# One layernorm tile moved beside a burst, and two blocks' softmax totals sent through DRAM, in a one-core attention and LoRA kernel

## The chip, the cores and the metric

The kernel runs on one core of a Trainium2 chip. Its time is the device time of that core in microseconds (us), as the median of several runs. A profile is one further execution, recorded by the hardware profiler; its times count from the start of its span. Five engines work side by side: TensorE (PE, with its weight loads as PEld), VectorE (DVE), ScalarE (ACT), GpSimd (POOL) and SyncE (SP), which here issues the DMAs. Each engine takes its instructions strictly in the order in which the program lists them.

## The reference

The input is four sequences of 1024 rows with 1024 columns, all in float32. Two steps follow each other:

```python
x = x + attention(layernorm(x), wq, wk, wv, wo)     # 32 heads of 32 columns, rotary q and k, causal softmax
x = x + lora(layernorm(x), route_w, A, Bw)          # one of 8 experts per row by its largest logit, rank 16

# inside attention, per head
probs = softmax(where(causal, q @ k.T / sqrt(32), lowest))
out = probs @ v
```

The weights are 1024x1024, the experts' matrices 8x16x1024 and 8x1024x16.

## The kernel before, in words

**Units.** The attention is cut into 32 units: four sequences `b` with eight groups `g` of four heads (4 x 32 = 128 columns). Unit u is group u % 8 of sequence u // 8, so unit 7 is the last of the first sequence. While unit u has its scores and softmax done, the projections (q, k, v) of unit u + 1 and, from the second sequence on, pieces of the output projection of the sequence before are put between. These go into a list of steps, `between[u]`, which is worked off during unit u. A step has a cost, in units of one 128x512 matmul; the loop over units (L1074) takes steps from the list, `todo`, until a slot's share of the cost is used (`fill`, `do_some`). A step of cost 0 has no matmul, and is done when its turn in the list comes. Nothing else decides the order: the program is written out in Python, and every engine follows it.

**Slots of a unit.** Queries are taken in 16 tiles t of 64 rows, in two blocks: block 0 is t = 0 to 7, block 1 is t = 8 to 15. `SLOTS` (L26) gives the order: score rounds for tiles 7 and 6, then 5, 4 and 3, then "second", then 2, 1, 0 and 9, then 15, 14, 13, 12, then "first", and then 11, 8 and 10. A score round (L417) runs its matmuls into the one PSUM tile `s` (L430), which ACT copies out (L441); POOL adds the causal mask (L444); DVE takes the maxima (L462) and joins the two halves of each row (L483); ACT takes the exponentials with their sums (L491); and DVE transposes the probabilities in place (L516). "second" (L1088) is `apply(u - 1, 1)`, the product of the probabilities of block 1 of the unit before with its values; "first" is `apply(u, 0)`. Such a product is a burst of 128 small matmuls per piece (L632), into the same PSUM tile `s`, so that the next score round can't start until DVE has read the burst's result (L652). Between the pieces of the second burst runs `meanwhile` (L1094): the transpose of v, and, where there is an entry `ahead_of[u]`, the moments of one layernorm tile of the next sequence (`find`). The entry's second half, the scaling of that tile (`scale`, L189), is run one slot later (L1113).

**Totals.** The softmax sums of a block are joined and inverted by `join_sums` (L555 to L566), and must then be spread over the rows on which the burst leaves its result. There are two ways. In the one (`by_turning` true), POOL widens the reciprocals into a 128x512 tile `by` (L569), PE transposes it in four matmuls (L603), and ACT copies it back (L604). In the other, DVE transposes 128x32 numbers (L576), four DMAs put them into DRAM (L582), and four more read them back, broadcast, into `by` (L587); both sets are put into `postponed`, with costs 2 and 5, and so are issued a few steps later, or at the latest by `spread_sums`. `by` has one buffer. In both ways L652 multiplies the burst's result by `by`.

**Layernorm ahead.** The eight 128-row tiles of the next sequence are normalized during this one (`Norm`, L247): `load`, `find` (two statistics instructions L178, an aggregate L180, an addition L182 on DVE, a power on POOL L184), `scale` (L189 on DVE), and `turn` (eight PE transposes L201, two copies L203 and L205 on ACT). For the second sequence, tiles 0 to 5 are found and scaled in units 1 to 6 by `ahead_of`; tile 6 and tile 7 are found and scaled in unit 6 by steps in `last_v`, which is `between[6]` (L923 to L930), tile 7 after steps 5 and 7 of the last v projection. Tiles 4 to 7 are turned in unit 7 by `change_steps` (L867).

Of the kernel before, what the change touches and what calls it, by code (L numbers as in the profile page):

```python
# [57 lines left out]
def weave(main, other):  # L58

    if not other:  # L60
        return list(main)
    out, taken = [], 0
    for n, step in enumerate(main):
        out.append(step)
        due = (n + 1) * len(other) // len(main)
        out += other[taken:due]
        taken = due
    return out + list(other[taken:])
# [3 lines left out]
def tile_preln_attn_then_top1_lora(  # L72
# [24 lines left out]
    NG = HEADS // HG  # L97
    NC = D // P
    NT = S // P
# [110 lines left out]
    units = [(b, g) for b in range(B) for g in range(NG)]  # L210
# [338 lines left out]
    def by_turning(u, blk):  # L549


        at = u + blk
        return at == 0 or at % NG == NG - 1 or at >= len(units) or (u, blk) == (NG - 2, 0)

    def join_sums(u, blk):  # L555

# [10 lines left out]
        if by_turning(u, blk):  # L567
            by = big.tile([P, TB, P], F32, tag="by", name=f"by_{u}_{blk}")
            nc.gpsimd.tensor_copy(  # L569
                by.rearrange("p t (h d) -> p t h d", d=HD),  # L570
                rec.rearrange("p h t -> p t h").unsqueeze(3).to_broadcast([P, TB, HG, HD]),
            )
            bys[u, blk] = by, None
            return
# [273 lines left out]
    def change_steps(u, norm, project, tail, held):  # L848

        p, h, turning, scaling = project, held, norm.turning, norm.scaling
        out, chains = [], []
        for n, tb in (("q", 0), ("k", 0), ("q", 1), ("k", 1), ("v", 0), ("v", 1)):
            chains += chain(u, n, tb)
        if p:
            turn, route, turn_hidden, adapt = tail
            find = norm.finding
            load_last = Step(lambda: norm.load(7), 0.0)
            out += [*h[:2], turn, *h[2:4], find(3), p[0], h[4], turning(2), h[5], p[1], route, scaling(3)]  # L860
            out += [find(4), h[6], p[2], h[7], p[3], turn_hidden, scaling(4), *p[4:6], adapt, load_last]
            out += [p[6], find(5), p[7], turning(3), scaling(5), *p[8:10], turning(4), *p[10:12]]
            chains = weave(chains[:-6], p[12:]) + chains[-6:]
            out += [*chains[:2], find(6), *chains[2:4], scaling(6), turning(5), *chains[4:6], find(7)]
            out += [*chains[6:8], scaling(7), turning(6), *chains[8:14], turning(7)]
            return out + chains[14:]
        for t, n in zip(range(TB, NT), (3, 4, 4, 4)):  # L867
            out += [*chains[:n], turning(t)]
            del chains[:n]
        return out + chains  # L870
# [4 lines left out]
    def behind(steps, at, step):  # L875

        steps.insert(steps.index(at) + 1, step)

    norms, ahead_of = {}, {}
    between, late_fetch = [], {}  # L880
    tail = []
    for u, (b, g) in enumerate(units):
        project, new_tail = [], []
        if b:
            fetch, (project,), new_tail = finish_steps(
                b - 1, g, "resident" if u == len(units) - 1 else "stream"
            )
            if g:
                apart = 3 if g + 1 == NG and u + 1 < len(units) else 8
                between[-1].insert(max(0, len(between[-1]) - apart), fetch)  # L890
            else:
                late_fetch[u] = fetch

        if u + 1 < len(units) and g + 1 == NG:
            last_v = between[-1]
            if b:
                norm = Norm(b + 1, {0: (2,), 2: (5,), 3: (6,)}, {3: "q", 4: "k", 6: "q"})
                load = [Step(lambda norm=norm, t=t: norm.load(t), 0.0) for t in range(2)]  # L900
                for at, step in (
                    (own["k", 0][0], load[0]),
                    (own["v", 0][0], norm.finding(0)),
                    (own["v", 0][1], load[1]),
                    (own["v", 0][2], norm.scaling(0)),
                    (own["v", 0][4], norm.finding(1)),
                    (own["v", 0][6], norm.turning(0)),
                    (own["v", 0][7], norm.scaling(1)),
                    (own["k", 1][2], norm.finding(2)),
                    (own["k", 1][3], norm.turning(1)),  # L910
                    (own["k", 1][5], norm.scaling(2)),
                ):
                    behind(last_v, at, step)
            else:

                norm = Norm(b + 1, {0: (7,)}, {5: "chunk", 6: "chunk"})
                for t in range(NG - 2):
                    ahead_of[t + 1] = (
                        lambda norm=norm, t=t: norm.find(t),
                        lambda norm=norm, t=t: norm.scale(t),  # L920
                    )
                    between[t].append(Step(lambda norm=norm, t=t: norm.load(t), 0.0))
                for at, step in (  # L923
                    (own["q", 0][0], Step(lambda norm=norm: norm.load(6), 0.0)),
                    (own["q", 1][0], norm.finding(6)),
                    (own["q", 1][3], norm.scaling(6)),
                    (own["v", 1][5], norm.finding(7)),
                    (own["v", 1][7], norm.scaling(7)),
                ):
                    behind(last_v, at, step)  # L930
                for t, at in enumerate((("k", 1), ("k", 1), ("k", 1), ("v", 1))):
                    behind(last_v, own[at][(1 + 3 * t) % NC], norm.turning(t))
            steps = change_steps(u + 1, norm, project, tail, held)
            norms[b + 1] = norm
        else:
            steps = []
            held = []
            if u + 1 < len(units):


                ends = g + 2 == NG and b + 1 < B
                own = {}
                for n, tb in ENDING if ends else USUAL:
                    own[n, tb] = chain(u + 1, n, tb)
                    if ends and b and (n, tb) == ("v", 1):
                        held = own[n, tb]
                    else:
                        steps += own[n, tb]
            if not steps:
                steps = list(project)  # L950
            elif b and not g:
                steps = steps[:36] + weave(steps[36:], project)
            else:
                steps = weave(steps[:-6], project) + steps[-6:]
            if u + 1 == len(units):
                new_tail6 = tail
            n = len(steps)
            for k, s in reversed(list(enumerate(tail))):
                steps.insert(6 + k * n // 7, s)
        between.append(steps)  # L960
        tail = new_tail
# [252 lines left out]
```

## Time and profile before

| | us |
|---|---|
| three runs | 2725.76, 2727.84, 2735.31 |
| median | 2727.84 |
| profiled execution | 2729.0 |
| its span, first to last instruction | 2727.2 |
| PE busy in the span | 2671.2 (98%) |
| DVE busy | 2141.2 (79%) |
| ACT busy | 1725.2 (63%) |
| POOL busy | 604.4 (22%) |
| mean granted PE clock | 0.995 |

The span is 1.8 us shorter than the execution. Unit 7 lies at some 515 to 592 us. The widening copies L569 of blocks (6, 0), (6, 1) and (7, 0), written as (unit, block), start at 498.58, 538.81 and 576.04 us. In a timeline a row gives the start, the time from the first to the last of a merged group, the engine, the line, the operation, the tiles and the count; in brackets stands the idle time before it, and who ended it.

### The profile page before, as it was taken

The numbers are of one execution on the slowest core, as the hardware profiler recorded it, in microseconds if no ns is written. First come the engines' busy times: TensorE is split into PE (matmuls) and PEld (weight loads), VectorE is DVE, ScalarE is ACT, GpSimd is POOL, SyncE is SP. The second block draws the span as 40 slices with busy tenths as digits, with TensorE's granted clock in tenths as the row PEclk, the third lists the DMA queues.
The fourth block names the chain that finished last, engine by engine and source line by source line (L and its number), as shares of the span: only waits on it lengthen the run. The fifth ranks groups of instructions, "written<-read, shape, count | busy, mean of one in ns | idle before, by whom it ended". The sixth has DMA issues, their size and how long they took to land.

```text
span 2727.2 us, 84063 instructions
## 1 busy us (share of the span) xinstructions
PE 2671.2 (98%) x35116; PEld 1305.0 (48%) x35116; DVE 2141.2 (79%) x4254; ACT 1725.2 (63%) x4980; POOL 604.4 (22%) x847
## 2 busy tenths in 40 slices
PE   8999999999999999989999999999999999999998
PEld 5444444444444544445444444444544444544445
DVE  4899999887777787887777878888778777777555
ACT  2878777876665676655666666766567666666421
POOL 2222222222221222222222222222212222222000
PEclk9999999999999999999999999999999999999999
DMA  3223233226555445652654444465354554446421
GB/s 118 60 72 74 75 77 84 53 56 174 139 140 131 126 131 155 167 157 61 163 161 134 135 131 132 136 187 142 83 159 135 159 136 133 131 132 185 123 69 53
DMA packets 465259, 332.19 MB, mean 122 GB/s; under 512 B 160496, under 2 KB 381936, under 8 KB 464880
## 3 DMA queue, kind: packets, MB, share of 16 engines
q1 hardware_dynamic: 464880, 326.83, 43.7%
q8 instruction: 276, 4.52, 0.7%
q14 instruction: 103, 0.84, 0.1%
HBM read 276.48 MB, written 50.24 MB: 120 GB/s over the span
## 4 chain that ended last, share of the span: by engine, by line
PE 79%; DVE 13%; ACT 3%; DMA 2%; POOL 1%; issue 1%; SPq 0%; POOLq 0%; DVEq 0%; ACTq 0%
PE po L749 15%; PE pq L337 14%; PE pk L337 13%; PE pv L337 11%; PE s L430 11%; PE av L632 8%; DVE top L462 4%; DVE pr L516 3%; PE ph L771 2%; PE pf L810 2%; ACT pr L491 1%; ACT pr L441 1%; DVE both L483 1%; PE pt_f L201 1%; DMA chunk<-in_wo 1%
## 5 line engine op out<-in xcount | busy, mean ns | idle before, releaser
L491 ACT ACTIVATE pr<-pr,both 128x256 f32<-128x256 f32 (+15 forms) x2048 | 1044.5, 519 | 55.5 <-DVE both L483 55.5
L441 ACT COPY pr<-s 128x640 f32<-128x640 f32 (+14 forms) x544 | 525.3, 1017 | 668.6 <-PE s L430 668.0
L462 DVE TENSOR_REDUCE top<-pr 128x2 f32<-128x960 f32 (+15 forms) x768 | 650.6, 893 | 256.8 <-POOL pr L444 256.2
L516 DVE STREAM_TRANSPOSE pr<-pr 128x1024 f32<-128x1024 f32 (+11 forms) x768 | 664.5, 907 | 33.7 <-ACT pr L491 30.4
L444 POOL TENSOR_TENSOR pr<-pr,causal_sb 128x128 f32<-128x128 f32 x512 | 239.0, 473 | 1152.2 <-ACT pr L441 1143.9
L337 PE MATMUL pv<-xnT,wv 128*128 128x512 f32 x1024 | 486.2, 602 | 0.0
L337 PE MATMUL pq<-xnT,wq 128*128 128x512 f32 x1008 | 479.1, 603 | 0.2 <-ACT xnT L203 0.2
L337 PE MATMUL pk<-xnT,wk 128*128 128x512 f32 x1008 | 476.8, 602 | 0.0
L430 PE MATMUL s<-kT,qT 32*32 32x256 f32 (+4 forms) x17408 | 393.8, 385 | 8.7 <-POOL pr L444 3.3
L491 ACT ACTIVATION_READ_ACCUMULATOR pr<-pr,both 128x1 f32 x2048 | 401.3, 196 | 0.0
L749 PE MATMUL po<-chunk,attn 128*128 128x512 f32 x736 | 379.7, 601 | 4.8 <-DMA chunk<-in_wo 4.8
L430 PEld LDWEIGHTS s<-kT,qT 32*32 32x32 f32 x17408 | 187.5, 103 | 266.2 <-issue 100.8
L337 PEld LDWEIGHTS pk<-xnT,wk 128*128 128x128 f32 x1008 | 181.2, 190 | 234.8 <-issue 234.5
L337 PEld LDWEIGHTS pq<-xnT,wq 128*128 128x128 f32 x1008 | 183.8, 192 | 226.1 <-issue 224.2
L337 PEld LDWEIGHTS pv<-xnT,wv 128*128 128x128 f32 x1024 | 185.6, 190 | 218.0 <-issue 217.2
L632 PE MATMUL av<-pr,vals 64*32 64x256 f32 (+3 forms) x12288 | 273.6, 321 | 6.9 <-DVE pr L516 6.5
L632 PEld LDWEIGHTS av<-pr,vals 64*32 64x32 f32 x12288 | 214.9, 106 | 115.5 <-issue 69.8
L483 DVE TENSOR_TENSOR both<-top 32x4 f32<-32x4 f32 (+3 forms) x1152 | 206.6, 179 | 23.8
L749 PEld LDWEIGHTS po<-chunk,attn 128*128 128x128 f32 x736 | 135.2, 190 | 170.1 <-issue 147.5
L652 DVE TENSOR_TENSOR at<-av,by 128x256 f32<-128x256 f32 x128 | 48.1, 417 | 110.0 <-PE av L632 71.5
L749 PE MATMUL po<-wo,attn 128*128 128x512 f32 x256 | 119.1, 607 | 2.3 <-DMA attn<-attn 2.3
L370 POOL TENSOR_TENSOR qT<-rawq,cos_sb 128x512 f32<-128x512 f32 x64 | 82.1, 1283 | 143.0 <-ACT rawq L363 143.0
(89 smaller groups left out, 1565.9 us busy)
## 6 DMA issues: line engine op xcount, KB each, us to landing
chunk<-in_wo SPq DMA_DIRECT2D x368, 256.0 KB, 3.8
vals<-vd SPq DMA_DIRECT2D x256, 128.0 KB, 4.3
x<-in_x SPq DMA_DIRECT2D x56, 512.0 KB, 5.0
wq<-in_wq SPq DMA_DIRECT2D x32, 512.0 KB, 4.7
wk<-in_wk SPq DMA_DIRECT2D x32, 512.0 KB, 3.9
wv<-in_wv SPq DMA_DIRECT2D x32, 512.0 KB, 4.2
vd<-vT SPq DMA_DIRECT2D x128, 128.0 KB, 4.5
out_y<-x SPq DMA_DIRECT2D x32, 512.0 KB, 2.6
```

The lines of the kernel that those rows point to most:

```text
L337: nc.tensor.matmul(at["p"], lhsT=wt[:, c, :], rhs=xnTs[b, tb][:, c, :], start=(c == 0), stop=(c == NC - 1),)
L370: nc.gpsimd.tensor_tensor(dst[:, cols], raw, cos_sb[:, cols], ALU.mult)
L430: nc.tensor.matmul(sc[i * SQ : (i + 1) * SQ, h, at : at + w].rearrange("p (j k) -> p j k", k=SQ), lhsT=of_q[rows, 2 * t + half], rhs=of_k[ ...
L441: nc.scalar.copy(pr[:, :, k0 : k0 + w], sc[:, :, at : at + w])
L444: nc.gpsimd.tensor_tensor(diagonal, diagonal, causal_sb.unsqueeze(1).to_broadcast([P, HG, SQ]), ALU.add)
L462: nc.vector.tensor_reduce(top[:, k, h : h + step], places[u, t][:, h : h + step, :], AX.X, ALU.max, negate=True,)
L483: nc.vector.tensor_tensor(dst[rows], src[rows], src[other], op)
L491: nc.scalar.activation(pr[:, h, :], pr[:, h, :], AF.Exp, bias=tops[u, t][:, h : h + 1], accum_out=dens[u, t // QT][:, t % QT, h : h + 1],)
L516: nc.vector.transpose(pr, pr)
L632: nc.tensor.matmul(avs[half][h * HD : (h + 1) * HD, t0:, :], lhsT=v[rows, j, h * HD : (h + 1) * HD], rhs=rhs, start=(j == 0), stop=(j == n ...
L749: nc.tensor.matmul(st["po"], lhsT=lhsT, rhs=rhs, start=(c == start), stop=(c == stop))
L771: nc.tensor.matmul(ph, lhsT=st["ynT"][:, c, :], rhs=w[:, c - i * RA, :], start=(c == 0), stop=(c == NC - 1),)
```

## The change

Two things are changed. In the first sequence (u < 8), only blocks (0, 0) and (6, 0) are still spread by turning; (6, 1) and (7, 0), which were too, now go by DRAM. And tile 7 of the second sequence's layernorm is no longer found and scaled by steps of `between[6]`, but by an entry `ahead_of[7]`: found between the two pieces of the burst (6, 1), in unit 7, and scaled in the slot after it. Its load stays where it was, after tile 0 is turned.

```diff
@@ by_turning(u, blk)
         at = u + blk
-        return at == 0 or at % NG == NG - 1 or at >= len(units) or (u, blk) == (NG - 2, 0)
+        if u < NG:
+            return (u, blk) in ((0, 0), (NG - 2, 0))
+        return at % NG == NG - 1 or at >= len(units)
@@ the loop that builds between[], b == 0, g + 1 == NG
                 norm = Norm(b + 1, {0: (7,)}, {5: "chunk", 6: "chunk"})
-                for t in range(NG - 2):
-                    ahead_of[t + 1] = (
+                for v, t in (*((t + 1, t) for t in range(NG - 2)), (NG - 1, NT - 1)):
+                    ahead_of[v] = (
                         lambda norm=norm, t=t: norm.find(t),
                         lambda norm=norm, t=t: norm.scale(t),
                     )
-                    between[t].append(Step(lambda norm=norm, t=t: norm.load(t), 0.0))
+                    if v < NG - 1:
+                        between[t].append(Step(lambda norm=norm, t=t: norm.load(t), 0.0))
                 for at, step in (
                     (own["q", 0][0], Step(lambda norm=norm: norm.load(6), 0.0)),
                     (own["q", 1][0], norm.finding(6)),
                     (own["q", 1][3], norm.scaling(6)),
-                    (own["v", 1][5], norm.finding(7)),
-                    (own["v", 1][7], norm.scaling(7)),
                 ):
```

## The prediction

> **What bounds the kernel now.** I read the page's busy times and chain first, then PE's waits by stretch, then the chain in order of time around unit 7, and then the timelines of PE, DVE, ACT, POOL and SP there. Units 4 and 5 serve as patterns, since they already do what unit 7 will do.
>
> ```profile
> PE 2671.2 (98%) x35116; PEld 1305.0 (48%) x35116; DVE 2141.2 (79%) x4254; ACT 1725.2 (63%) x4980; POOL 604.4 (22%) x847
> PE 79%; DVE 13%; ACT 3%; DMA 2%; POOL 1%; issue 1%; SPq 0%; POOLq 0%; DVEq 0%; ACTq 0%
> ```
>
> PE is the bound, so something off PE gains only where PE waits. Of the 13% of the chain that DVE has, a part lies where the change is. PE's timeline shows it:
>
> ```profile
> 520.28 1.44 PE L430 MATMUL s<-kT,qT 32*32 32x256 f32 x64 [2.70 <-ACT pr L441]
> 521.65 4.52 PE L337 MATMUL pq<-xnT,wq 128*128 128x512 f32 x6
> ...
> 532.09 1.04 PE L201 MATMUL pt_a<-eye_sb,x 128*128 128x128 f32 x8
> 537.04 6.43 PE L632 MATMUL av<-pr,vals 64*32 64x256 f32 x128 [3.91 <-DVE pr L516]
> ```
>
> PE stands 3.91 us until DVE has transposed block (6, 1), and the burst's first piece then takes 6.43 us. In unit 5 the same piece takes 3.68 us (start 329.92, no idle). The excess of 2.75 us is the clock, by the table of windows (third column from the end):
>
> ```profile
> 534.00:537.00 3.00, 0.00 (x0) 0.00 (x0) 2.90 (x7) 2.41 (x9) 0.00 (x0) 0.72 0.00 0
> 537.00:540.00 3.00, 2.96 (x53) 2.24 (x61) 2.84 (x8) 2.49 (x10) 0.61 (x1) 0.50 0.00 0
> 540.00:543.00 3.00, 3.00 (x80) 2.54 (x68) 2.89 (x8) 0.99 (x4) 0.00 (x0) 0.65 0.03 5
> ```
>
> What DVE does before it lets PE go:
>
> ```profile
> 525.87 0.67 DVE L483 TENSOR_TENSOR both<-top 32x8 f32<-32x8 f32 x4
> 526.57 1.29 DVE L178 BATCH_NORM_STATS2 st_a<-x 128x6 f32<-128x512 f32 x2
> 527.89 0.21 DVE L180 BATCH_NORM_AGGREGATE mv_a<-st_a 128x2 f32<-128x12 f32 x1
> 528.14 0.15 DVE L182 TENSOR_SCALAR ve_a<-mv_a 128x1 f32<-128x1 f32 x1
> 528.96 0.94 DVE L189 TENSOR_SCALAR x<-x,mv_a,rstd_a 128x1024 f32<-128x1024 f32 x1 [0.67 <-POOL rstd_a L184]
> 529.82 1.82 DVE L516 STREAM_TRANSPOSE pr<-pr 128x768 f32<-128x768 f32 x2
> 531.57 2.16 DVE L462 TENSOR_REDUCE top<-pr 128x4 f32<-128x1024 f32 x2
> 533.77 0.73 DVE L483 TENSOR_TENSOR both<-top 32x8 f32<-32x8 f32 x4
> 534.52 3.02 DVE L516 STREAM_TRANSPOSE pr<-pr 128x704 f32<-128x704 f32 x4
> ```
>
> The five middle instructions are tile 7's layernorm, with a trip to POOL, and DVE has no other idle time from there to the burst. They lie on the chain.
>
> **The change, part by part.**
>
> *Layernorm taken from before the burst.* DVE's next work starts at 526.57 instead of 529.82, so 3.25 us earlier. Its inputs allow it: ACT ended tile 11's exponentials at 523.5, and POOL's masks for tiles 7 and 6, which stood behind the waiting power (POOL idle 7.61 us until 528.37), can run at about 526. Carrying on: transposes of tile 11 to 528.3, maxima to 530.5, their joining to 531.2, the two transposes of tile 10 (about 0.83 each of the 3.02) to 532.9, the first of tile 8 to 533.6. The last needs tile 8's fourth exponential, which ACT gives only at 533.7, behind an eviction that has no part in the change:
>
> ```profile
> 531.45 1.85 ACT L441 COPY pr<-s 128x768 f32<-128x768 f32 x3
> 533.19 0.55 ACT L491 ACTIVATE pr<-pr,both 128x288 f32<-128x288 f32 x1
> ```
>
> So the last transpose ends at about 534.5 instead of 537.54: 3.0 of the 3.25 us arrive, and ACT is the next limit. PE is free at 533.13, starts its first heads at 533.6 and waits shortly for the last two until 534.5, in all 1.0 to 1.4 us idle instead of 3.91. At 3.5 us for the rest the piece ends at 538.0 instead of 543.47: **5.5 us**, of which 3.0 is the earlier transpose and 2.5 the clock.
>
> The clock's part rests on a rule, and here row and rule differ. The Trainium skill (TensorE: Matmul & The Clock Gate, the table "Why this matters for your kernels") asks for no PE-idle gap over about 3 us, since one idle window drops the clock to half. In this trace the gap of 2.70 us at 517.6 was enough: granted clock 0.50 from 522 to 524, and six matmuls took 4.52 us where six otherwise take 2.84. By rule and row alike a remaining gap of 1.0 to 1.4 us keeps the full clock (gaps of 0.97 and 1.31 us, at 475 and 408, had no such stretch). But if only half of the shift arrived, leaving some 2.4 us, the rule would still give 1.5 + 2.5 = 4.0 us and the row only 1.5. I take the row for the range.
>
> *The same layernorm put beside the burst.* Five DVE instructions (1.29 + 0.21 + 0.15, later 0.94) and POOL's power (0.55). DVE after the burst's start, by the durations of before: sums and reciprocal to 535.6, the new 128x32 transpose (0.21) to 535.8, maxima 2.21 and joining 0.69 to 538.8, transpose of tile 7 to 540.0, of v to 541.2, the moments to 542.9, shuffle and product to 544.4. PE meanwhile: 2 + 4 matmuls to 540.8, second piece to 543.1, 2 matmuls, a turn and 4 matmuls (0.86 + 0.88 + 1.72) to 546.5, where the score round of tiles 2, 1, 0, 9 needs DVE to have read the burst: L652 from 544.4 to 545.2, 1.3 us in time. What hides the moments is idle time that DVE had here before (1.27 + 2.76 + 3.20 us between 543.9 and 555.6). Scaling ends at about 548.1; tile 7 is turned at 550.4 (before: 556.32). Cost nothing; if the cover were gone, at most the 2.6 us themselves.
>
> *Totals of (6, 1) by DRAM.* Removed: POOL 0.61, four PE transposes, ACT 0.59, and DVE's 2.76 us wait for that copy. The Trainium skill (same page, "Part 4: PE-mode transpose") measured about 275 ns for one transpose in a kernel's context. The row has the same, 273 ns, but the four overlap: in the chain they take 0.59 us. By the rule eight of them are 2.2 us, by the row 1.2; I take the row, **0.6 us** a block. Added: eight DMAs on SP, 0.41 us of issue each. Put and get stand behind the unit-8 wk load (issued 517.61) and ahead of the attn store, which waits for L652 anyway; SP is otherwise idle from 518 to 550. How long the trip takes, unit 5 shows:
>
> ```profile
> 330.83 1.71 SPq L582 DMA_DIRECT2D recs<-recT  x4
> 333.56 2.25 SPq L587 DMA_DIRECT2D by<-recs  x4
> 339.89 0.34 SPq L665 DMA_DIRECT2D attn<-at  x1
> ```
>
> From the small transpose's end (330.8) to the last landing (335.8 + 2.2 = 338.0) are 7.2 us; in unit 6 it is 8.1. From 535.8 that is 543.0 to 543.9, before DVE comes to L652 at 544.4. Cost nothing.
>
> *Totals of (7, 0) by DRAM.* Again 0.6 us of PE. The small transpose ends at 576.1 of the old clock, landing at 583.3 to 584.2; DVE comes to L652 at 585.2, busy until then. Behind put and get on SP now stands the wq load of unit 9, issued some 5 us later than 576.74; with 4.7 us to land it is there by 586.5, and its first matmul was at 597.92.
>
> After that PE has no idle time in unit 7 or 8's start, so what is gained stays. **Sum: 5.5 + 0.6 + 0.6 = 6.7 us.** Against the profiled execution's 2729.0 (span 2727.2, 1.8 outside) that is 2722.3. The median of the runs is 1.2 lower, so 2721.1; I forecast **2721.5**.
>
> **Bounds.** PE idle before the burst (3.91), clock excess (2.75) and transposes (1.2) give at most 7.9 us in this place. At least the transposes and half of the shift: 1.2 + 1.5 = 2.7. Later half-clock stretches (the trace's clock record falls to half for 3.4 us at four more places, all after 1200 us) depend on where a gap falls against the gate's windows; shifting all by 6.7 us may add or remove one or two, some 1.7 us each (half of 3.4), either way.
>
> **The rivals.**
> - *ACT or the clock keeps part of it (20%)*: ACT's fourth exponential comes later than I put it, PE still idles over 2 us and the clock still falls. 2.7 to 4 us gained, about 2724.5. For it: ACT already sets the end, 0.2 us after DVE would. Against: its work before that point is not touched.
> - *Everything comes, and a later half-clock stretch goes as well (10%)*: 9 to 11 us, about 2718.
> - *It does not act at all (5%)*: PE is 98% busy, and what DVE gains is waited for elsewhere; only transposes are saved, 2727. Against: the chain runs through these very instructions.
> - *Slower (6%)*: DVE waits in L652 for the DRAM trip of (6, 1), behind it wait the scaling of tile 7 and the tops, and PE's next score round. It decides against the change from the moment that the landing is later than 552.4 (546.5 less 0.75 for L652, plus the 6.7 gained), 16.6 us after the small transpose. With every issue and landing at the worst of all 212 (1.58 and 3.5, 1.81 and 3.8 us): 4 x 1.58 + 3.5 + 4 x 1.81 + 3.8 = 20.9, landing 556.7: 11.0 us of wait less 6.7 gained, 4.3 us slower than before, about 2732. Against: 53 such trips in the trace, and PE waited at most 0.97 us for one.
> - The forecast itself: 59%.
>
> **Numbers.** The range is 2715.5 to 2727: from the third case's deeper part to the lower bound of the first with the runs' scatter of some us. Over 0.5% (13.6 us, about what a measurement of this kernel can tell from no change) would be below 2714.2 or above 2741.5; no single mechanism above reaches either. Faster 0.06, same 0.91, slower 0.03.
>
> **What would show it.** After: PE's idle before the first piece of (6, 1) at most 1.5 us instead of 3.91, that piece at 3.7 to 4.4 us, no stretch of half clock there; DVE goes from L483 straight to L516; the wait of L652 for ACT's copy is gone with no DMA wait over 1 us in its place; units 0 to 6 as before. Wrong, if the clock still falls at 535, if PE waits for DVE at the score round near 546, or if the span moves by more than this place does.

## The result and the profile after

| | before | after |
|---|---|---|
| median, us | 2729.38 (7 runs, 2725.76 to 2735.31) | 2721.73 (7 runs, 2716.47 to 2724.26) |
| profiled execution, its span | 2729.0, 2727.2 | 2722.25, 2720.5 |
| mean granted PE clock | 0.995 | 0.997 |

The ratio of after to before is 0.997, with a 95% interval of 0.996 to 0.998: 5.5 to 10.9 us less. That is within half a per cent, as forecast, and 0.2 us from the forecast of 2721.5. The text below shows that the terms of the sum came less exactly than that.

In the changed kernel the lines behind L553 stand two further down: L632 is L634, L652 is L654. PE's timeline at the same place, and DVE's ahead of it:

```profile
521.54 1.62 PE L430 MATMUL s<-kT,qT 32*32 32x256 f32 x64 [2.69 <-ACT pr L441]
523.09 4.32 PE L337 MATMUL pq<-xnT,wq 128*128 128x512 f32 x6
...
533.32 1.04 PE L201 MATMUL pt_a<-eye_sb,x 128*128 128x128 f32 x8
535.32 0.64 PE L634 MATMUL av<-pr,vals 64*32 64x256 f32 x8 [0.96 <-DVE pr L516]
536.20 3.66 PE L634 MATMUL av<-pr,vals 64*32 64x256 f32 x120 [0.25 <-DVE pr L516]
```

```profile
527.12 0.92 DVE L483 TENSOR_TENSOR both<-top 32x8 f32<-32x8 f32 x4
528.08 1.84 DVE L516 STREAM_TRANSPOSE pr<-pr 128x768 f32<-128x768 f32 x2
529.84 2.17 DVE L462 TENSOR_REDUCE top<-pr 128x4 f32<-128x1024 f32 x2
532.04 0.73 DVE L483 TENSOR_TENSOR both<-top 32x8 f32<-32x8 f32 x4
532.80 2.37 DVE L516 STREAM_TRANSPOSE pr<-pr 128x704 f32<-128x704 f32 x3
535.37 0.78 DVE L516 STREAM_TRANSPOSE pr<-pr 128x576 f32<-128x576 f32 x1 [0.20 <-ACT pr L491]
```

The layernorm is gone from before the burst, DVE goes straight on, and the last transpose waits 0.20 us for ACT's fourth exponential: ACT is the next limit, as forecast. POOL's masks for tiles 7 and 6, which stood behind the waiting power until 528.88 before, begin at 526.26. PE's idle time at the burst is 0.96 + 0.25 us instead of 3.91, and the first piece runs at full clock (granted clock 1.00 from 535 to 540). After the burst began:

```profile
542.72 1.25 DVE L178 BATCH_NORM_STATS2 st_a<-x 128x6 f32<-128x512 f32 x2
544.00 0.21 DVE L180 BATCH_NORM_AGGREGATE mv_a<-st_a 128x2 f32<-128x12 f32 x1
544.24 0.15 DVE L182 TENSOR_SCALAR ve_a<-mv_a 128x1 f32<-128x1 f32 x1
...
545.09 1.72 DVE L371 TENSOR_TENSOR swapq<-swapq,sin_sb 128x512 f32<-128x512 f32 x1
546.73 0.74 DVE L654 TENSOR_TENSOR at<-av,by 128x256 f32<-128x256 f32 x2
```

L654 shows no wait in brackets: the DRAM trip of (6, 1) was there before DVE was. PE's next score round starts at 548.49, 1.0 us after L654 ends, with no idle time either.

**A measure for the place.** Two executions don't reach 508 us at the same time (the changed one is 1.27 us later there, with nothing changed so far). So I count from the score round of tile 11 in unit 6 to that of unit 7, start to start on PE, and call it the stretch: 586.37 - 508.25 = 78.12 us before, 581.99 - 509.52 = 72.47 after. **5.65 us are won in this place.** The two rounds, before and then after:

```profile
508.25 1.49 PE L430 MATMUL s<-kT,qT 32*32 32x384 f32 x64
...
586.37 1.49 PE L430 MATMUL s<-kT,qT 32*32 32x384 f32 x64
```

```profile
509.52 1.48 PE L430 MATMUL s<-kT,qT 32*32 32x384 f32 x64
...
581.99 1.50 PE L430 MATMUL s<-kT,qT 32*32 32x384 f32 x64
```

The profiled spans differ by 6.7: 1.27 was lost ahead of it and 2.3 won behind it, where the clock's record has four spells of half clock before (at 1201, 2559, 2645 and 2686 us) and two after (1881 and 2680). The last section has more on these.

### The profile page after: what moved, and what is told of

The parts are those of the page before. It is cut to its first block, busy times and chain, and to the rows that moved or that the text cites. A ratio compares the mean times of both kernels' runs of the same rounds, so it can differ in the third digit from the quotient of the medians.

```text
span 2720.5 us, 84063 instructions
## 1 busy us (share of the span) xinstructions
PE 2666.9 (98%) x35108; PEld 1302.4 (48%) x35108; DVE 2143.7 (79%) x4256; ACT 1723.5 (63%) x4978; POOL 601.4 (22%) x845
## 3 DMA queue, kind: packets, MB, share of 16 engines
q8 instruction: 276, 4.52, 0.7%
## 4 chain that ended last, share of the span: by engine, by line
PE 79%; DVE 13%; DMA 3%; ACT 3%; POOL 1%; issue 1%; SPq 1%; POOLq 0%; DVEq 0%; ACTq 0%
PE po L751 15%; PE pq L337 14%; PE pk L337 13%; PE pv L337 11%; PE s L430 11%; PE av L634 8%; DVE top L462 4%; DVE pr L516 3%; PE ph L773 2%; PE pf L812 2%; DMA chunk<-in_wo 2%; DVE both L483 1%; ACT pr L441 1%; ACT pr L491 1%; PE pt_f L201 1%
## 5 line engine op out<-in xcount | busy, mean ns | idle before, releaser
L634 PE MATMUL av<-pr,vals 64*32 64x256 f32 (+3 forms) x12288 | 272.0, 319 | 4.6 <-DVE pr L516 3.8
L634 PEld LDWEIGHTS av<-pr,vals 64*32 64x32 f32 x12288 | 214.1, 106 | 112.3 <-issue 66.4
L483 DVE TENSOR_TENSOR both<-top 32x4 f32<-32x4 f32 (+3 forms) x1152 | 207.8, 180 | 23.8
L654 DVE TENSOR_TENSOR at<-av,by 128x256 f32<-128x256 f32 x128 | 48.2, 418 | 108.7 <-PE av L634 70.4
L375 POOL TENSOR_TENSOR qT<-qT,swapq 128x512 f32<-128x512 f32 x64 | 81.6, 1274 | 140.0 <-DVE swapq L371 140.0
```

The lines of the kernel that those rows point to most:

```text
L375: nc.gpsimd.tensor_tensor(dst[:, cols], dst[:, cols], other, ALU.add)
L483: nc.vector.tensor_tensor(dst[rows], src[rows], src[other], op)
L634: nc.tensor.matmul(avs[half][h * HD : (h + 1) * HD, t0:, :], lhsT=v[rows, j, h * HD : (h + 1) * HD], rhs=rhs, start=(j == 0), stop=(j == n ...
```

## The experiments

Theory: the layernorm lay on DVE's chain before the burst; most of the gain is its moving, part of it through the clock. Rival 1: the totals by DRAM do it. Rival 2: the first piece is slow for another reason than the clock. Rival 3: the layernorm still costs something in its new place. The ratios are to runs of the kernel before that were taken alongside on the same chip.

**Layernorm alone** (`by_turning` as before):

```diff
-        if u < NG:
-            return (u, blk) in ((0, 0), (NG - 2, 0))
-        return at % NG == NG - 1 or at >= len(units)
+        return at == 0 or at % NG == NG - 1 or at >= len(units) or (u, blk) == (NG - 2, 0)
```

> Layernorm of tile 7 moved beside the burst; all totals spread as before. The measure is the stretch from the score round of tile 11 in unit 6 to that in unit 7 (start to start on PE): 78.1 us before, 72.5 after the whole change. Theory (the layernorm lay on DVE's chain before the burst): stretch near 73.5, so 4.6 of the 5.6 us, no half clock at the burst of (6, 1). Rival (the totals do it: no wait of L652 for ACT's copy): stretch stays at 77 to 78. Median: 4 to 7 us under before by the theory, 0 to 1 by the rival.

Measured: stretch 73.21 us, 4.91 less; ratio 0.9973 (0.9963 to 0.9982). The piece again takes 3.7 us at full clock:

```profile
531.87 0.64 PE L632 MATMUL av<-pr,vals 64*32 64x256 f32 x8 [0.95 <-DVE pr L516]
532.75 3.66 PE L632 MATMUL av<-pr,vals 64*32 64x256 f32 x120 [0.25 <-DVE pr L516]
```

**Totals alone** (the kernel before with the new `by_turning`):

> Only the totals of (6, 1) and (7, 0) by DRAM; tile 7 normalized before the burst as before. Theory: only the eight transposes go, 0.6 us a block, stretch near 77.0, idle before the burst still 3.9 us and the clock still at half there. Rival (the totals do it): stretch near 73. If the DRAM trip costs a wait, the stretch is over 78. Median within 2 us of before by the theory.

Measured: stretch 77.41, 0.71 less; ratio 0.9992 (0.9986 to 0.9998), so 0.5 to 3.8 us. Rival 1 falls. That 4.91 and 0.71 add up to nearly 5.65 is partly chance: of the 0.71, 0.53 come from a first piece that ended earlier (34.69 us into the stretch instead of 35.22), with one spell of half clock of 3.41 us there instead of 6.83, and a new wait at (7, 0) takes 0.29 back. A cleaner price of the totals is the layernorm alone against the whole change, where the clock holds in both: 73.21 - 72.47 = 0.74 us. The DRAM way also shows its risk here, at (7, 0):

```profile
578.67 3.15 SPq L589 DMA_DIRECT2D by<-recs  x4
```

```profile
535.89 5.91 PE L634 MATMUL av<-pr,vals 64*32 64x256 f32 x128 [4.15 <-DVE pr L516]
...
584.52 1.48 PE L430 MATMUL s<-kT,qT 32*32 32x384 f32 x64 [0.61 <-DVE at L654]
```

The four reads took 3.15 us to issue instead of 1.70 in the whole change, and PE waited 0.61 us at the score round behind them. Slow issue is not needed for such a wait: in three other runs (half of the shift, and the totals of (6, 0) by DRAM with no and with four spare matmuls) the four reads took 1.70 us, and PE still waited 0.32, 0.16 and 0.17 us at that round. The piece of (6, 1) keeps its idle time and its half clock.

**Tile 7's layernorm left out** (that tile is projected unnormalized):

```diff
+                    if v == NG - 1:
+                        ahead_of[v] = (
+                            lambda norm=norm: setattr(norm, "found", NT),
+                            lambda norm=norm: setattr(norm, "scaled", NT),
+                        )
```

> The whole change with the moments and the scaling of the second sequence's tile 7 left out altogether, so that tile goes into the projections unnormalized. It prices the layernorm in its new place. Theory (idle time of DVE hides it): stretch within 0.3 us of the whole change's 72.5, median within 1.5 us of it. Rival (it still costs its 2.6 us on DVE, which paces PE's next score round): stretch near 70.

Measured: stretch 72.43; median 2721.99, ratio 0.9971 (0.9961 to 0.9982). In its new place the layernorm costs 0.04 us (72.47 - 72.43). DVE instead waits 0.94 us for the DRAM trip, so the time that hides it is there either way; rival 3 falls.

```profile
544.34 0.76 DVE L654 TENSOR_TENSOR at<-av,by 128x256 f32<-128x256 f32 x2 [0.94 <-DMA by<-recs]
```

**Half of the shift** (the moments stay before the burst, the scaling moves):

```diff
                     (own["q", 1][3], norm.scaling(6)),
+                    (own["v", 1][5], norm.finding(7)),
```

> As the whole change, but the moments of tile 7 (1.65 us on DVE) stay before the burst, and only the scaling with its wait for POOL goes beside it, so half of the shift. PE's idle before the burst near 2.2 us. If the clock only falls after a gap over about 3 us, as the rule has it, no half clock at the burst, and a stretch near 74. If a gap of 2.1 to 2.7 us is enough, as the row at 517 us has it, half clock there and a stretch near 76.5. Median 4 under before by the rule, 1 to 3 by the row.

Measured: stretch 75.91; ratio 0.9978 (0.9972 to 0.9985). But PE's idle time was 4.47, not 2.2:

```profile
518.12 1.44 PE L430 MATMUL s<-kT,qT 32*32 32x256 f32 x64 [2.70 <-ACT pr L441]
519.49 2.84 PE L337 MATMUL pq<-xnT,wq 128*128 128x512 f32 x6
...
533.76 5.79 PE L634 MATMUL av<-pr,vals 64*32 64x256 f32 x128 [4.47 <-ACT pr L491]
```

The gap of 2.70 us at 515 to 518 was this time *not* followed by half clock (six matmuls in 2.84 us), so PE was at the burst earlier and waited longer. The row names ACT as the releaser, but DVE too worked without a gap until its last transpose ended at 534.27; the burst starts 27.67 us into the stretch, 1.1 earlier than before. As a test of the two readings of the clock it misses. It shows something else: PE's idle time before the burst is not a size of its own. The softmax work on DVE and ACT sets when the burst starts, and PE's arrival varies with the clock before.

**Spare matmuls where PE waits, in the kernel before**:

```diff
         avs, pieces = value_pieces(u, blk)
+        for k in range(7 if (u, blk) == (NG - 2, 1) else 0):
+            if k == 0:
+                spare = bank([P, HALF], f"spare_{u}_{blk}")
+            nc.tensor.matmul(spare, lhsT=eye_sb, rhs=cos_sb[:, :HALF], start=True, stop=True)
```

> The kernel before with seven spare 128x512 matmuls (some 3.1 us, into a bank that nothing reads) where PE waits before the first piece of (6, 1), so that PE is busy there while DVE's chain is untouched. If the slow first piece (6.4 us instead of 3.7) is the clock's doing, that piece takes 3.7 to 4.2 us, no half clock there, and the stretch is 78.1 - 2.5 = 75.6. If it is slow for another reason (the transposes of the last two heads, bank or memory contention), it stays at 5.8 to 6.4 and the stretch at 78. Median 2 to 3 under before by the first.

```profile
532.79 6.17 PE L1057 MATMUL spare<-cos_sb,eye_sb 128*128 128x512 f32 x14
538.90 3.69 PE L632 MATMUL av<-pr,vals 64*32 64x256 f32 x128
```

Measured: the piece takes 3.69 us, which speaks against rival 2, though the piece also started later. But a float32 matmul is two rows in the profile; seven took 6.17 us and held the burst up by some 1.8. The stretch is 77.16, ratio 0.9992 (0.9985 to 0.9999).

**Three spare matmuls instead of seven:**

> The kernel before with three spare 128x512 matmuls (six rows of the profile, 2.7 us; seven were 6.2 us and held the burst up) in PE's idle 3.9 to 5.5 us ahead of the first piece of (6, 1). By the clock theory the idle time left is 1.2 us after a half-clock stretch at 520, or some 2.8 without one; in the first case the burst starts 28.8 us into the stretch as before, takes 3.7 us, and the stretch is 78.1 - 2.7 = 75.4. If the slow piece is not the clock's doing, 78.

```profile
531.31 2.74 PE L1057 MATMUL spare<-cos_sb,eye_sb 128*128 128x512 f32 x6
535.41 4.22 PE L632 MATMUL av<-pr,vals 64*32 64x256 f32 x128 [1.36 <-DVE pr L516]
```

Measured: the burst starts 28.78 us into the stretch, as before (28.79), and its first piece ends at 33.00 instead of 35.22: **the clock alone is 2.2 us** here, and with the same start rival 2 falls. The stretch is 76.94 and not the 75.4 expected: the piece takes 4.22 us, not 3.7, and PE stands still once more for 0.87 us inside the burst of (7, 0), with no releaser in the profile. Ratio 0.9984 (0.9977 to 0.9991).

**A better version?** The totals of (6, 0) by DRAM too:

```diff
-            return (u, blk) in ((0, 0), (NG - 2, 0))
+            return (u, blk) in ((0, 0),)
```

> The whole change, and the totals of (6, 0) by DRAM too. Theory: the gap of 2.7 us before the score round of tile 10 starts with DVE's wait of 2.3 us for ACT's copy of (6, 0); by DRAM the landing comes 7.5 us after the small transpose, 1.0 to 1.5 us before ACT's copy would, so the gap shrinks to some 1.5 us and the half clock after it goes: 0.5 + 1.2 + 1.7 = 2.5 to 3.5 us under the whole change, about 9 under before. Rival (the trip is no faster than the copy, and DVE waits as long for the DMA): 0 to 1 us under the whole change.

Measured: the gap before tile 10's round shrinks to 1.11 us and the burst of (6, 1) starts 1.6 us earlier in the stretch; but PE, no longer slowed, waits 2.57 us for it, and now the clock falls there:

```profile
518.76 1.43 PE L430 MATMUL s<-kT,qT 32*32 32x256 f32 x64 [1.11 <-POOL pr L444]
520.12 2.84 PE L337 MATMUL pq<-xnT,wq 128*128 128x512 f32 x6
...
532.49 5.77 PE L634 MATMUL av<-pr,vals 64*32 64x256 f32 x128 [2.57 <-DVE pr L516]
```

Stretch 72.14; ratio 0.9968 (0.9955 to 0.998), not to be told from the whole change. The median of its five runs, 2718.5, lies some 3 us lower, as expected, but the stretch only 0.3. So I filled the waits ahead of the first pieces of (0, 1) and (6, 1), first with four spare matmuls each, then with two.

**With four spare matmuls:**

> The whole change, the totals of (6, 0) by DRAM as well, and four spare matmuls (1.8 us) ahead of the first pieces of (0, 1) and (6, 1), where PE waits 2.6 us for DVE. If the earlier start by the one is spoilt by the half clock that it brings (first piece 5.8 us there), the first piece takes 3.7 us, the stretch is 72.1 - 2.1 = 70.0, unit 1 gains 2 us more, and the median is 3 to 5 us under the whole change, with less scatter. If not, it is as the run without the spare matmuls.

Measured: stretch 73.79, where 70.0 was expected; ratio 0.9972 (0.996 to 0.9984). Four took 3.6 us and held the burst up by some 2; and this time DVE waited for the trip of (6, 0):

```profile
503.24 0.76 DVE L654 TENSOR_TENSOR at<-av,by 128x256 f32<-128x256 f32 x2 [2.87 <-DMA by<-recs]
```

**With two spare matmuls:**

> The whole change, the totals of (6, 0) by DRAM, and two spare matmuls (1.8 us) ahead of the first pieces of (0, 1) and (6, 1). Theory: no window of 3.4 us is idle for 1.9 us there any more, so both first pieces take 3.7 to 4 us; stretch 72.1 - 2.1 = 70.0 if the landing of (6, 0) is in time as in the one trace, 71.5 if it is 1.5 us late as in the other. Median 2 to 5 us under the whole change, 8 to 11 under before. If the spare matmuls hold up the bursts again, as the whole change.

Measured: no half clock in units 1 to 7, stretch 71.61; ratio 0.997 (0.9957 to 0.9983). The stretch is the best of all; the median, 2720.82, is not 2 to 5 us under that of the whole change (2721.73) as expected.

**The whole change once more:**

> The whole change once more, beside the other three on one chip. Median 5 to 8 us under before. The stretch 72.5 if the gap before (6, 1), near 1.2 us, keeps the clock again; 74 to 75 if the clock falls this time.

Measured: stretch 72.48; ratio 0.9976 (0.9966 to 0.9986). Yet PE's idle time before the burst was 2.60, not 1.2, and the clock held, both there and after the gap of 2.69 us at 517:

```profile
519.73 1.44 PE L430 MATMUL s<-kT,qT 32*32 32x256 f32 x64 [2.69 <-ACT pr L441]
521.10 2.84 PE L337 MATMUL pq<-xnT,wq 128*128 128x512 f32 x6
...
533.51 0.64 PE L634 MATMUL av<-pr,vals 64*32 64x256 f32 x8 [2.60 <-DVE pr L516]
```

**The whole change, with two spare matmuls ahead of (0, 1) alone:**

> The whole change with two spare matmuls (1.8 us) ahead of the first piece of (0, 1) alone, where PE waits 2.6 us and the clock falls in most executions. Theory: no half clock at 135 us, the score round of tile 11 in unit 6 starts near 506 us in every execution instead of 506 to 509.5, and the median is 1 to 2 us under the whole change. Stretch 72.5 as there.

Measured: no half clock at 135 us, stretch 72.51, but the score round of tile 11 is at 506.92, no earlier than in several others (506.07 with the layernorm alone); ratio 0.9959 (0.9944 to 0.9974), median 2718.68. The best ratio of all, with an interval that overlaps the whole change's, so it is not shown to be faster than it.

## Why the prediction was right

- *Right: the layernorm lay on the chain, and ACT is the next limit.* Forecast: the last transpose 3.0 us earlier. Measured from the stretch's start: it ends at 29.29 before (537.54) and 26.63 after (536.15), 2.7 us. Most of the 0.3 us missing is one slower station, the joining L483 (0.92 instead of 0.67, while POOL masks): ACT's exponentials wait for it, and ACT then works without a gap to the last one that the burst needs.
- *Right in kind, a little large: the clock.* Forecast 2.5 us; the kernel before with three spare matmuls measures 2.2. The whole change has 4.88 instead of 5.5 in all until the first piece ends (35.22 to 30.34).
- *Too large: the transposes.* Forecast 0.6 us a block from their place in the chain. Measured: from the first piece's end to the score round of tile 2, 9.02 before and 8.63 after, and from the burst of (7, 0) to tile 11's round, 7.16 and 6.78: 0.4 each, and 4.88 + 0.39 + 0.38 is the 5.65. The place in the chain was itself too large: the four transposes hold PE for 0.50 us from their start to the next matmul's, not 0.59, and without them the pair of matmuls behind the burst takes 0.96 to the next start instead of 0.86. Before, then after:

```profile
548.45 0.66 PE L603 MATMUL pr<-eye_sb,by 128*128 128x128 f32 x4
548.95 1.02 PE L337 MATMUL pk<-xnT,wk 128*128 128x512 f32 x2
```

```profile
544.84 1.13 PE L337 MATMUL pk<-xnT,wk 128*128 128x512 f32 x2
```

- *Right: the new place costs nothing, and the DRAM trips little.* The layernorm costs 0.04 us there. The trips of (6, 1) and (7, 0) were in time in the changed kernel's trace; but in four of the nine traces with these trips PE waited for (7, 0), 0.16 to 0.61 us, where the forecast had the trip landed 1.0 to 1.9 us before DVE needed it. The slower case, a landing over 16.6 us after the small transpose, came nowhere near: the longest wait of DVE for such a trip in units 6 and 7 of the runs was 2.87 us.
- *Wrong: how the clock's rule was put.* The prediction set a gap over 3 us against a gap of 2.7 that had been enough, and counted on 1.0 to 1.4 us being left. Neither reading holds (last section), and the remaining gap is 1.2 or 2.6 us by execution. That the result stood in both is due to where the gaps lie, which the prediction did not see; that its 1.0 to 1.4 us came out in the first trace was luck. It also missed a fifth further spell of half clock in the trace before, at 136 us, ahead of the place.
- *The total* fits better than its terms, by luck: the place gave 5.65 us instead of 6.7, while the median before rose from 2727.84 (three runs) to 2729.38 (seven), so that the medians differ by 7.65 with an interval from 5.5. When the changed kernel ran again its ratio gave 6.5 us (3.8 to 9.3), and that interval holds 5.65. A difference of 2 us behind the place is within what one or two later spells of half clock do, so I don't ascribe it to the change; it is not settled. The prediction also took 13.6 us to be about what runs of this kernel can tell from no change; these intervals are some 5 us wide and leave out zero.

## What to carry to other kernels

A step that PE doesn't need soon can still be on PE's path, if it stands in the queue of the engine that PE waits for next; look for it in the chain in order of time, and move it behind that wait, where the engine is idle. Before counting a wait's length, ask who sets its end: time given to the engine that arrives early only makes it wait longer. Compare profiled executions by a stretch between two equal instructions, not by their spans.

## What the runs showed of the hardware

- *The clock falls by the idle time within a fixed window.* Within each trace the spells of half clock begin on a grid of 3.41 us, and last one or two of its windows. Of 109 PE-idle gaps of 1.9 us or more in all 13 traces, 57 were followed by one and 52 not, at the same lengths (2.5 to 3 us: 16 of 25). Laying the grid over the traces sorts them. Of all windows, those with PE idle for less than 1.7 us were followed by half clock in 6 of 10,217 cases, those with 1.7 to 2.0 us in 10 of 27, and those with more in 56 of 57. So a gap that a window's edge splits in the middle is free, and one that lies within a window costs 1.7 us (six matmuls at 521.65 in the trace before, 4.52 us instead of 2.84) to 2.2 us (the first piece of (6, 1)). It is why the gap of 2.60 us before (6, 1) did no harm when the changed kernel ran again: an edge at 532.13 splits it into 1.23 and 1.38. The gap at 517 there lies some 13.8 us, about four windows, earlier, and is split too, at 518.48. It is the same in the two other traces that have both gaps behind the whole shift (tile 7's layernorm left out, and spare matmuls ahead of (0, 1)). In the changed kernel's first trace, 2.28 us of the gap at 519 lie in one window; half clock follows, and makes PE so late for the burst that only 1.2 us of waiting are left. It is also a part of why the same kernel's runs scatter by 8 to 12 us: of 46 runs of the kernel before, the nine with a granted clock of 0.997 took 2727.0 us in the mean and the nine with 0.994 took 2731.6. In 32 others the relation is weak, so how large a part is open.
- *A DVE product takes longer while a POOL product runs.* The product L371 takes 0.69 us alone and 1.72 in the changed kernel (545.09 to 546.81), where POOL's L370 runs from 544.99 to 546.26: it ends 0.55 us after POOL does. In the trace before it takes 1.09 us and ends 0.54 after. The rows before, and then POOL's after:

```profile
545.24 1.28 POOL L370 TENSOR_TENSOR qT<-rawq,cos_sb 128x512 f32<-128x512 f32 x1 [5.82 <-ACT rawq L363]
545.97 1.09 DVE L371 TENSOR_TENSOR swapq<-swapq,sin_sb 128x512 f32<-128x512 f32 x1
```

```profile
544.99 1.27 POOL L370 TENSOR_TENSOR qT<-rawq,cos_sb 128x512 f32<-128x512 f32 x1
```

That fits the Trainium skill (SBUF — State Buffer, "Terms"), by which the two share a pair of ports that one instruction holds to its end. The prediction had 0.8 us for this product, and L654 kept 1.0 instead of 1.3 us to the next score round.
